# Two attention layers and two feed-forward layers in one kernel: a fourth buffer for transposed contexts, another order of the first loads, and a shorter chain of work before the last layer

## The chip, the cores and the metric

The kernel runs on one core of one Trainium2 chip. The metric is device time in microseconds (us) for one execution; lower is better. The core has TensorE (matmuls, PE in the profile, with its weight loads as PEld), VectorE (DVE), ScalarE (ACT), GpSimd (POOL) and SyncE (SP), which only issues transfers. Each engine works off its own instructions in the order in which the program gives them, and waits on semaphores for what others produce. Transfers are issued by SP, ScalarE and GpSimd, and 16 DMA engines carry them out.

## What is computed

There are 16 batches, each of 112 query rows and 375 context rows of 256 numbers, all in 32-bit floats. Four layers follow one another, each as `x = x + layer(layernorm(x))`:

```python
def _L0_xattn_ref(patch_embed, pixel_embed, Wq, Wk, Wv, Wo, bo):   # 16 heads of 64
    q = patch_embed @ Wq
    k = pixel_embed @ Wk
    v = pixel_embed @ Wv
    ...
    attn = jax.nn.softmax(sim, axis=-1)
    ...
    return out @ Wo + bo
def _L0_ffn_ref(...):                                  # 2 experts, one per row, and a shared one
    top1 = jnp.argmax(gate_probs, axis=-1)
    ...
    h = jax.nn.relu(jnp.einsum('end,edh->enh', masked, w1) + b1[:, None, :])
    expert_out = jnp.einsum('enh,ehd->end', h, w2) + b2[:, None, :]
    ...
    shared = jax.nn.relu(xf @ sw1 + sb1) @ sw2 + sb2
    return (routing_output + shared).reshape(B, S, D)
def _L1_xattn_ref(query, key, value, mask):            # one head of 256, key = value = context
    e = jnp.einsum('bid,bjd->bij', query, key) * scale
    ...
    a = jax.nn.softmax(e, axis=-1)
    return jnp.einsum('bij,bjd->bid', a, value)
def _L1_ffn_ref(x, weight_int8, weight_scale, bias):   # one scale for all of x
    x_scale = jnp.maximum(jnp.abs(x2).max() / 127.0, EPS)
    x_int8 = jnp.clip(jnp.round(x2 / x_scale), -128, 127).astype(jnp.int8)
    ...
    out = acc_i32.astype(jnp.float32) * x_scale * weight_scale.T
```

The last layer needs the largest absolute value over all 16 batches before it can quantize anything.

## The kernel before

The order of all work is written out by hand: a list of units, and for each unit calls that are put in its middle (`mid`) or at its end (`at`). What is issued first on an engine or a queue runs first there.

*The opening* (L137 to L187, L1169 to L1174). SP and ScalarE issue the first loads: x of the first two batches (`load_xb`, 224 KB) and the transposed context of batch 0 (`ctxT`, 375 KB), then the weights wk, wq and wv in quarters of 256 KB (`first_w`). While these come in, TensorE runs `WARM` products of zeros (L182). Then follow the first keys (`make_kT`, L338, L347), the turn of x (`q_turn`, L327, L330), and the first queries (`make_q`, L395).

*The first attention* (units 0 to 63, `unit`). A unit is four heads of one batch. Unit u computes the scores of u (L426), their largest values on VectorE (L434), exponentials on ScalarE (L443), the division on GpSimd (L455), and the keys of unit u + 1. The values of unit u - 2 (`make_v`, L359) are made in unit u, and unit u - 3 gets its weighted sum (L514). So the values of unit 0 are made in unit 2.

*Shared and routed feed-forward.* The shared expert runs in seven chunks of 256 rows (`Rows.run`, L760 for the first layer, L772 on ScalarE and L770 on VectorE for the relu `hT`, L747 for the second layer). For the two experts the rows are sorted into slots of 128 rows, in two halves of the batches. A slot's result is stored in HBM (`slot_store`, L823, tensor y_s) by SP. Rows are gathered back by GpSimd (`sort_get`, L829, tile got) when all slots of the half are stored, and are added to x (L843).

*The last eight batches* (TAIL = 8, batches 8 to 15) go through the second attention after the first has ended. The driver is `stages(k)`. Step k runs the scores of batch 8 + k (`second_2`, L857, tile pe), with the softmax (L862, L871, L872 and L878), the turn of the probabilities (`second_3`, L460), and the weighted sum of the batch two steps behind (`second_4`, L888). The layer norm before it is L271 and L272 on VectorE, L275, L276 and L286 on GpSimd and L300 on ScalarE; the norm after it is followed by a turn (`third_turn`, L327, L330) and the batch's largest value (`third_max`, L925). In the units before step 0, the last chunk of the shared expert, number 6, runs in four parts on TensorE, between the norms of batches 8 and 9. Its result is stored to x2_d by SP (L804), and from there x of batches 13 to 15 is loaded (L809).

Each batch needs two forms of its context: `ctxT2` (L130, transposed, 128 partitions) for the scores and `ctx_nat` (L121, 125 partitions of three rows) for the weighted sum. In this stage `ctxT2` has three buffers and `ctx_nat` five. Pairs 8, 9 and 10 are issued on SP's queue one per unit, each after the store of a slot; the later ones at the end of steps 0 to 4. `x3T` (L1244, 896 KB) brings back what batches 0 to 7 have ready for the last layer, on the same queue.

*The end* (L1328 to L1399). The largest value of batch 15 comes straight from its statistics (`farthest`). It is turned on TensorE (pm), reduced on VectorE (top), spread over all partitions by a product (pb), with two small products between them that keep TensorE going (`keep_warm`). From it come xscale and rscale. Then pairs of batches are scaled (`scaled`, L1355 on ScalarE or L1357 on VectorE), made whole numbers (`products`, L1362), multiplied (L1366), scaled back (L1377), added to x (L1385, on VectorE or GpSimd) and stored by SP (L1386). The tile y has four buffers.

Of the kernel before, what the change touches and what calls it, by code (L numbers as in the profile page):

```python
# [9 lines left out]
F32 = mybir.dt.float32  # L10
# [9 lines left out]
P = 128  # L20
B, S, D = 16, 112, 256
SK = 375
# [4 lines left out]
DC = D // P  # L27
MC = INNER // P
FC = HID // P
GB = 2  # L30
# [11 lines left out]
QB = S // 4  # L42
KB = (SK + 31) // 32
KP = (P, P, SK - 2 * P)
WARM = 4
POOL_PLACES = 7
CROW_PLACES = 4
NT = B * S // P
# [6 lines left out]
TAIL = 8  # L55
# [3 lines left out]
def tile_kernel(  # L59
# [26 lines left out]
    nc = tc.nc  # L86
# [4 lines left out]
    ctxp = ctx.enter_context(tc.tile_pool(name="ctx", bufs=2))  # L91
# [19 lines left out]
    xb = {}  # L111

    def load_xb(g):
        xb[g] = tmp.tile([S, GB, D], F32, tag="xb", name=f"xb_{g}", bufs=1)
        (nc.gpsimd if g else nc.sync).dma_start(out=xb[g], in_=x[:, g * GB : (g + 1) * GB, :])

    ctx_nat, ctxT, ctxT2 = {}, {}, {}

# [5 lines left out]
    def load_ctxT(b, dma=nc.sync):  # L124
        ctxT[b] = ctxp.tile([P, DC, SK], F32, tag="ctxT", name=f"ctxT{b}")
        dma.dma_start(out=ctxT[b], in_=ctx_t[b])

    def load_ctxT2(b):
        ctxT2[b] = late(ctxp, 2, 3, [P, DC, SK], "ctxT_2", f"ctxT2_{b}")
        nc.sync.dma_start(out=ctxT2[b], in_=ctx_t[b])  # L130

    def weight(src, name, dma, pool=wpool):
        t = pool.tile(list(src.shape), F32, tag=name, name=name)
        dma.dma_start(out=t, in_=src)
        return t

    load_xb(0)  # L137
    load_ctxT(0, nc.scalar)
    first_w = {
        n: awpool.tile([P, DC, INNER], F32, tag=n, name=n) for n in ("wk", "wq", "wv")  # L140
    }
    for k in range(UN):
        sl = slice(k * UD, (k + 1) * UD)
        for n, src, dma in (("wk", wk, nc.sync), ("wq", wq, nc.scalar), ("wv", wv, nc.sync)):
            dma.dma_start(out=first_w[n][:, :, sl], in_=src[k])
        if k == 0:

            ones = const.tile([P, P], F32, tag="ones", name="ones")
            nc.vector.memset(ones, 1.0)
            nc.scalar.activation(ones[0:1, 0:1], ones[0:1, 1:2], AF.Identity)  # L150
# [94 lines left out]
    def late(pool, bufs, more, shape, tag, name):  # L245

        pool, bufs = (fin[0], more) if fin else (pool, bufs)
        return pool.tile(shape, F32, tag=tag, name=name, bufs=bufs)
# [86 lines left out]
    def make_kT(b, m, on_act):  # L335
        pk = gen(f"pk_{b}_{m}")
        for dc in range(DC):
            nc.tensor.matmul(  # L338
                pk[:, :SK],
                wk_sb[:, dc, m * P : (m + 1) * P],  # L340
                ctxT[b][:, dc, :],
                start=(dc == 0),
                stop=(dc == DC - 1),
            )
        t = act.tile([P, SK], F32, tag="kT", name=f"kT_{b}_{m}", bufs=2)
        if on_act:
            nc.scalar.copy(t, pk[:, :SK])  # L347
        else:
            nc.vector.tensor_copy(t, pk[:, :SK])
        kT[b, m] = t  # L350
# [562 lines left out]
    def third_turn(bs):  # L913
        for b in bs:
            if b < TAIL:
                t = tmp.tile([P, DC, S], F32, tag="x3s", name=f"x3s_{b}", bufs=1)
                transposed(t, normed["l3", b], f"x3_{b}")
                nc.scalar.dma_start(out=x3T_d[b], in_=t)
            else:
                transposed(x3T[0][:, b, :, :], normed["l3", b], f"x3_{b}")  # L920
# [90 lines left out]
    NU = B * UN  # L1011
# [6 lines left out]
    def at(u, f, *a):  # L1018
        extra[u].append((f, a))
# [142 lines left out]
    for b in range(TAIL, B):  # L1162

        at(FIRST_RUN + 3 if b < 13 else STEP_0 + b - 13, load_xs, b)
    for i in range(3):
        at(STEP_0 - 7 + i, load_ctxT2, TAIL + i)
        at(STEP_0 - 7 + i, load_ctx, TAIL + i)

    make_kT(0, 0, True)  # L1169
    for i in range(GB):  # L1170
        q_turn(0, i)
    make_kT(0, 1, True)
    for m in range(2):
        make_q(0, m)  # L1174

    def unit(u, work=None):
        nb, nk = divmod(u + 1, UN)
        vb, vk = divmod(u - 2, UN)
        has_s = u < NU
        has_k = u + 1 < NU  # L1180
        has_t = 0 <= u - 1 < NU
        has_v = 0 <= u - 2 < NU
        has_w = 0 <= u - 3 < NU
        after_block = u - 1 in blocks
        if has_w and after_block:
            weighted(u - 3)
        if has_t:
            unit_T(u - 1, 0)
            unit_T(u - 1, 1)
        if has_s:  # L1190
            scores(u)
            exps(u, 0)
            exps(u, 1)
        if has_w and not after_block:
            weighted(u - 3)
        if has_t:
            unit_T(u - 1, 2)
            unit_T(u - 1, 3)
            stay = unit_move(u - 1)
        pump(3)  # L1200
        if has_k:
            make_kT(nb, 2 * nk, True)
        if has_s:
            divide(u, 0)
        pump(3)
        if has_v:
            make_v(vb, vk, (0, 1))
        pump(4)
        for f, a in middle[u]:
            f(*a)  # L1210
        if has_s:
            divide(u, 1)
        if work:
            work()
        pump(4)
        if has_k:
            make_kT(nb, 2 * nk + 1, True)
        if has_v:
            make_v(vb, vk, (2,))
        if has_t:  # L1220
            unit_stay(*stay)
        pump(4)
        for f, a in extra[u]:
            f(*a)
            pump(2)

    def keep_warm(count):

        pi = gen("warm")
        for _ in range(count):  # L1230
            nc.tensor.matmul(pi[:, :P], ident, ident, start=True, stop=True)
# [22 lines left out]
    def stages(k):  # L1254
        def b_of(back):
            b = TAIL + k - back
            return b if TAIL <= b < B else None

        def do(back, f):
            b = b_of(back)  # L1260
            if b is not None:
                f(b)

        def norm_steps(name, b):
            nb_on = nc.gpsimd if name == "l2" or b == B - 1 else nc.vector
            steps[name, b] = norm([b], name, True, nb_on)
            for f in steps[name, b][:3]:
                f()

        def now(f, at_k):  # L1270

            for b, own in zip(range(TAIL, B), at_k):
                if own == k:
                    f(b)

        def rows(name):
            return lambda b: steps[name, b][3]()

        no = None
        stats = lambda b: norm_steps("l2", b)  # L1280
        now(sort_get, (-4, -4, -3, -3))
        now(sort_add, (-3, -3, no, no, 1, 2, 3, 4))
        now(stats, (-2,))
        now(rows("l2"), (-1,))
        yield
        now(sort_add, (no, no, -2, -1))
        now(stats, (no, -2))
        if k == -1:
            now(rows("l2"), (no, -1))
            do(-1, second_1)  # L1290
        do(0, lambda b: second_2(b, lambda: do(-1, second_1)))
        do(4, lambda b: third_turn([b]))
        do(1, second_3)
        do(3, rows("l3"))
        now(rows("l2"), (no, no, 0, 1, 2, 3, 4, 5))
        do(2, second_4)
        if k == B - TAIL + 1:

            amax1.append(const.tile([S, 1], F32, tag="amax1", name="amax1"))
            do(3, lambda b: third_max([b]))  # L1300
            nc.vector.tensor_reduce(amax1[0], amax[:, : B - 1], AX.X, ALU.max)
        do(2, lambda b: norm_steps("l3", b))
        now(sort_get, (no, no, no, no, -1, 0, 1, 2))
        now(stats, (no, no, -1, 0, 1, 2, 3, 4))
        if k >= 0:
            do(-3, load_ctxT2)
            do(-3, load_ctx)
        if k != B - TAIL + 1:
            do(3, lambda b: third_max([b]))
        yield  # L1310
# [22 lines left out]
    nc.tensor.transpose(pm[:1, :S], amax1, ident[:S, :S])  # L1333
    top = const.tile([1, 1], F32, tag="top", name="top")
    nc.vector.tensor_reduce(top, pm[:1, :S], AX.X, ALU.max)
    keep_warm(2)
    pb = gen("pb")
    nc.tensor.matmul(pb[:, :1], ones[0:1, :], top, start=True, stop=True)
    xscale = const.tile([P, 1], F32, tag="xscale", name="xscale")
# [11 lines left out]
    def scaled(pair):  # L1351
        t = x3T[0][:, 2 * pair : 2 * pair + 2, :, :]

        if pair % 2 or pair == 6:
            nc.scalar.activation(t, t, AF.Identity, bias=rounding, scale=rscale)  # L1355
        else:
            nc.vector.tensor_scalar(t, t, rscale, ROUND, ALU.mult, ALU.add)  # L1357
# [17 lines left out]
    def stored(pair):  # L1375
        y = fin[0].tile([S, 2, D], F32, tag="y", name=f"y_{pair}", bufs=4)
        nc.vector.tensor_tensor(  # L1377
            y,
            pfs[pair][:S, : 2 * D].rearrange("p (j d) -> p j d", j=2),
            wsx.unsqueeze(1).to_broadcast([S, 2, D]),  # L1380
            ALU.mult,
        )
        first = xs_place[2 * pair]
        add = nc.vector if pair in (2, 5, 7) else nc.gpsimd
        add.tensor_tensor(y, y, xall[:S, first : first + 2, :], ALU.add)  # L1385
        nc.sync.dma_start(  # L1386
            out=out[2 * pair : 2 * pair + 2].rearrange("b s d -> s b d"), in_=y
        )
# [70 lines left out]
```

## Time and profile before

| What | us |
|---|---|
| median of 3 runs (lowest, highest) | 969.3 (968.51, 970.0) |
| the profiled execution, whole time | 970.18 |
| its span, first to last instruction | 968.4 |
| TensorE busy in the span | 925.2 |
| VectorE, ScalarE, GpSimd busy | 494.3, 465.9, 463.8 |
| mean granted TensorE clock | 0.986 |

The page gives each engine's busy time over the whole span, and cuts the span into 40 slices of 24.2 us. The timelines quoted further down have one row for each instruction, or for several merged ones (x4): start in us from the span's start, length in us, engine, line, what it writes and reads, and in brackets how long the engine stood idle before it and what ended that. Rows of SPq are transfers that SP issues; their length is that of the issue, not of the transfer. Rows of stretches give for each engine its busy time in us and, in brackets, its instructions, then the clock granted to TensorE, the share of the 16 DMA engines that was busy, and the GB/s that they moved.

### The profile page before, as it was taken

To read this page: it belongs to the slowest core of one execution; us is meant where nothing else is said; L and a number is where in the kernel's file an instruction comes from. 1 tells how busy PE (TensorE), PEld (TensorE's weight loads), DVE (VectorE), ACT (ScalarE), POOL (GpSimd) and SP (SyncE) were. 2 spreads that over 40 slices of the span, in tenths; PEclk is the share of its full clock that TensorE was granted. 3 is DMA by queue.
4 is the path that set the end of the run, shared out by engine and by line. 5 is a ranking of instruction groups with operands and counts; after the bars stand their busy time and mean duration, and the time that the engine had idled before them with its cause. 6 is when DMAs were issued, how large, how long until landed. Compare 5 with 4: busy or idle time off the path is not lost. (4 is left out here: it accounts for less than half of the span.)

```text
span 968.4 us, 16839 instructions
## 1 busy us (share of the span) xinstructions
PE 925.2 (96%) x5567; PEld 706.4 (73%) x5567; DVE 494.3 (51%) x1276; ACT 465.9 (48%) x1241; POOL 463.8 (48%) x504
## 2 busy tenths in 40 slices
PE   8999999999999999999999999899999999999683
PEld 5677677777777777778778787667767678899462
DVE  5655855464545444653444434577576442322464
ACT  4766565366535554564353442554545641221453
POOL 4766664366536544553242334666555622201743
PEclk9999999999999999999999999999999999999996
DMA  5654543243326422332645522645335720586522
GB/s 185 161 164 95 136 129 74 71 101 92 74 74 197 121 70 52 77 83 59 217 159 179 205 50 70 161 127 139 95 77 133 201 59 30 201 325 220 151 96 76
DMA packets 119911, 120.69 MB, mean 125 GB/s; under 512 B 15807, under 2 KB 107153, under 8 KB 115089
## 3 DMA queue, kind: packets, MB, share of 16 engines
q1 hardware_dynamic: 107664, 97.52, 35.8%
q10 hardware_dynamic: 8144, 11.20, 4.0%
q0 software_dynamic: 4016, 10.90, 3.7%
q8 instruction: 45, 0.74, 0.3%
q14 instruction: 42, 0.34, 0.1%
HBM read 71.19 MB, written 10.62 MB: 84 GB/s over the span
## 5 line engine op out<-in xcount | busy, mean ns | idle before, releaser
L455 POOL TENSOR_SCALAR p<-p,rden 128x375 f32<-128x375 f32 x256 | 315.1, 1244 | 258.4 <-DVE rden L452 251.3
L443 ACT ACTIVATE p<-sc,nmax 128x375 f32<-128x375 f32 x256 | 143.4, 571 | 174.9 <-DVE nmax L434 169.6
L338 PE MATMUL pk<-ctxT,wk 128*128 128x375 f32 x512 | 192.1, 497 | 4.3 <-ACT kT L347 2.3
L359 PE MATMUL pv<-wv,ctxT 128*128 128x256 f32 (+1 forms) x768 | 187.0, 380 | 0.4 <-ACT kT L347 0.4
L359 PEld LDWEIGHTS pv<-wv,ctxT 128*128 128x128 f32 (+1 forms) x768 | 143.3, 187 | 47.9 <-ACT kT L347 1.6
L504 ACT COPY pT<-blk 32x384 f32<-32x384 f32 x256 | 130.0, 508 | 29.2 <-DMA pT<-blk 26.9
L476 DVE STREAM_TRANSPOSE blk<-p 128x384 f32<-128x384 f32 x256 | 132.2, 552 | 7.4 <-POOL p L455 4.5
L338 PEld LDWEIGHTS pk<-ctxT,wk 128*128 128x128 f32 x512 | 90.3, 191 | 55.7 <-issue 9.9
L434 DVE TENSOR_REDUCE nmax<-sc 128x2 f32<-128x750 f32 x128 | 111.8, 911 | 0.6 <-PE sc L426 0.5
L514 PEld LDWEIGHTS pa<-pT,v 128*64 128x64 f32 (+1 forms) x1536 | 74.4, 136 | 33.3 <-issue 15.8
L426 PE MATMUL sc<-kT,qT 64*128 64x375 f32 x512 | 98.1, 501 | 0.0
L514 PE MATMUL pa<-pT,v 128*64 128x112 f32 (+1 forms) x1536 | 88.3, 263 | 2.2 <-DMA pT<-blk 1.4
L372 DVE COPY v<-pv 119x256 f32<-119x256 f32 x64 | 27.0, 423 | 122.5 <-PE pv L359 101.3
L347 ACT COPY kT<-pk 128x375 f32<-128x375 f32 x128 | 61.3, 479 | 47.0 <-PE pk L338 47.0
L426 PEld LDWEIGHTS sc<-kT,qT 64*128 64x128 f32 x512 | 43.9, 186 | 34.1 <-issue 13.5
L770 DVE TENSOR_SCALAR hT_sl<-ph_sl,slot_b 128x128 f32<-128x128 f32 x64 | 22.3, 349 | 69.3 <-PE ph_sl L760 69.3
L760 PE MATMUL ph_sh<-ffn_x,sw 128*128 128x256 f32 x224 | 56.0, 381 | 0.0
L747 PE MATMUL acc_sh<-sw,hT_sh 128*128 128x256 f32 x224 | 55.5, 379 | 0.3 <-ACT hT_sh L772 0.3
L395 PE MATMUL pq<-xT,wq 128*128 128x224 f32 x256 | 54.2, 354 | 0.0
L772 ACT ACTIVATE hT_sl<-ph_sl,slot_b 128x128 f32<-128x128 f32 x64 | 23.2, 367 | 60.6 <-PE ph_sl L760 49.2
L443 ACT ACTIVATION_READ_ACCUMULATOR p<-sc,nmax 128x1 f32 x256 | 51.8, 202 | 0.0
L542 PE MATMUL po<-wo,oT 128*128 128x256 f32 x224 | 50.8, 380 | 0.1
(221 smaller groups left out, 1148.1 us busy)
## 6 DMA issues: line engine op xcount, KB each, us to landing
pT<-blk SPq DMA_DIRECT2D x732, 48.0 KB
ctxT<-in_ctx_t SPq DMA_DIRECT2D x31, 375.0 KB
ctx<-in_ctx SPq DMA_DIRECT2D x16, 375.0 KB
ew<-in_w ACTq DMA_DIRECT2D x2, 1024.0 KB
x_s<-idle POOLq DMA_DIRECT2D x2, 1024.0 KB, 5.8
sw<-in_sw ACTq DMA_DIRECT2D x2, 1024.0 KB
row<-x_s SPq DMA_DIRECT2D x16, 128.0 KB
y_s<-yrow SPq DMA_DIRECT2D x16, 128.0 KB
```

What stands on the lines that cost most here:

```text
L338: nc.tensor.matmul(pk[:, :SK], wk_sb[:, dc, m * P : (m + 1) * P], ctxT[b][:, dc, :], start=(dc == 0), stop=(dc == DC - 1),)
L347: nc.scalar.copy(t, pk[:, :SK])
L359: nc.tensor.matmul(pv[: KP[c], n * UD : (n + 1) * UD], ctxT[b][:, dc, c * P : c * P + KP[c]], wv_sb[:, dc, k * UD : (k + 1) * UD], start=( ...
L426: nc.tensor.matmul(sc[:, j, :SK], qT[g, m][r, i * P : (i + 1) * P], kT[b, m][r, :], start=True, stop=True,)
L434: nc.vector.tensor_reduce(nmax, sc[:, :, :SK], AX.X, ALU.max, negate=True)
L443: nc.scalar.activation(p[:, :SK], sc[:, j, :SK], AF.Exp, bias=nmax[:, j : j + 1], accum_out=den[:, j : j + 1])
L455: nc.gpsimd.tensor_scalar(p, p, rden[:, j : j + 1], None, ALU.mult)
L476: nc.vector.transpose(blocked[u][:, :, h * 32 : (h + 1) * 32], probs[u][h].rearrange("p (n k) -> p n k", k=32),)
L504: nc.scalar.copy(pT[r, :, i, :], of[r, :, i, :])
L514: nc.tensor.matmul(pa[j * DH : (j + 1) * DH, j2 * S : (j2 + 1) * S].rearrange("p (i q) -> p i q", q=QB), vv[b, k][: KP[c], c, h * DH : (h ...
L747: nc.tensor.matmul(self.acc[:n, i, :D], hT[:, i * n : (i + 1) * n], self.wb[:, f, :], start=(f == 0), stop=(f == FC - 1),)
L760: nc.tensor.matmul(ph[:, : self.n], self.wa[:, dc, f * P : (f + 1) * P], self.src[:, dc, :], start=(dc == 0), stop=(dc == DC - 1),)
```

## The change

- The first loads: batch 0's transposed context is loaded in two halves, one by SP and one by ScalarE. Then SP loads the first quarter of wk in two halves; x goes to ScalarE's queue, behind its half of the context. The number of warm-up products (`WARM`) goes from 4 to 3.
- The first unit: both keys come first, then the values of unit 0 (`make_v`), around the turns of x. Unit 2 makes no values any more.
- The contexts of the second attention: `ctxT2` gets four buffers in place of three. Pairs 8 and 9 are issued together, and 10 and 11 one unit later. Step k then loads batch 8 + k + 4 in place of 8 + k + 3. On SP's queue pairs 10 and 11 thereby stand ahead of the store of the last slot, and pair 12 stands where 11 stood.
- The end: batch 14's turn goes from the last step, behind pb, to the step before, ahead of pm. The two `keep_warm` products between top and pb are dropped. ScalarE scales pairs 2 to 7 (before 1, 3, 5, 6 and 7) and VectorE pairs 0 and 1. VectorE adds pairs 4 and 7 (before 2, 5 and 7), and GpSimd the others.

```diff
-WARM = 4
+WARM = 3
...
-        (nc.gpsimd if g else nc.sync).dma_start(out=xb[g], in_=x[:, g * GB : (g + 1) * GB, :])
+        (nc.gpsimd if g else nc.scalar).dma_start(out=xb[g], in_=x[:, g * GB : (g + 1) * GB, :])
...
-        ctxT2[b] = late(ctxp, 2, 3, [P, DC, SK], "ctxT_2", f"ctxT2_{b}")
+        ctxT2[b] = late(ctxp, 2, 4, [P, DC, SK], "ctxT_2", f"ctxT2_{b}")
...
-    load_xb(0)
-    load_ctxT(0, nc.scalar)
+    ctxT[0] = ctxp.tile([P, DC, SK], F32, tag="ctxT", name="ctxT0")
+    for c, dma in enumerate((nc.sync, nc.scalar)):
+        dma.dma_start(out=ctxT[0][:, c, :], in_=ctx_t[0][:, c, :])
     first_w = {
         n: awpool.tile([P, DC, INNER], F32, tag=n, name=n) for n in ("wk", "wq", "wv")
     }
+    for m in range(2):
+        sl = slice(m * P, (m + 1) * P)
+        nc.sync.dma_start(out=first_w["wk"][:, :, sl], in_=wk[0][:, :, sl])
+    load_xb(0)
     for k in range(UN):
         sl = slice(k * UD, (k + 1) * UD)
         for n, src, dma in (("wk", wk, nc.sync), ("wq", wq, nc.scalar), ("wv", wv, nc.sync)):
-            dma.dma_start(out=first_w[n][:, :, sl], in_=src[k])
+            if k or n != "wk":
+                dma.dma_start(out=first_w[n][:, :, sl], in_=src[k])
...
-    for i in range(3):
-        at(STEP_0 - 7 + i, load_ctxT2, TAIL + i)
-        at(STEP_0 - 7 + i, load_ctx, TAIL + i)
+    for i in range(4):
+        at(STEP_0 - 7 + i // 2, load_ctxT2, TAIL + i)
+        at(STEP_0 - 7 + i // 2, load_ctx, TAIL + i)
 
     make_kT(0, 0, True)
+    make_kT(0, 1, True)
+    make_v(0, 0, (0, 1))
     for i in range(GB):
         q_turn(0, i)
-    make_kT(0, 1, True)
+    make_v(0, 0, (2,))
     for m in range(2):
         make_q(0, m)
...
-        has_v = 0 <= u - 2 < NU
+        has_v = 0 < u - 2 < NU
...
-        do(4, lambda b: third_turn([b]))
+        if k < B - TAIL + 2:
+            do(4, lambda b: third_turn([b]))
...
             do(3, lambda b: third_max([b]))
             nc.vector.tensor_reduce(amax1[0], amax[:, : B - 1], AX.X, ALU.max)
+            do(3, lambda b: third_turn([b]))
...
         if k >= 0:
-            do(-3, load_ctxT2)
-            do(-3, load_ctx)
+            do(-4, load_ctxT2)
+            do(-4, load_ctx)
...
-    keep_warm(2)
...
-        if pair % 2 or pair == 6:
+        if pair > 1:
...
-        add = nc.vector if pair in (2, 5, 7) else nc.gpsimd
+        add = nc.vector if pair in (4, 7) else nc.gpsimd
```

## The prediction

> **What bounds the kernel now.** I read the page first: TensorE is busy for 96% of a span of 968.4 us, so time is lost only where TensorE stands or runs at a lower clock. The slices show this in the first, in the last three, and nowhere else.
>
> ```profile
> PE 925.2 (96%) x5567; PEld 706.4 (73%) x5567; DVE 494.3 (51%) x1276; ACT 465.9 (48%) x1241; POOL 463.8 (48%) x504
> PE   8999999999999999999999999899999999999683
> PEclk9999999999999999999999999999999999999996
> ```
>
> Then TensorE's timeline at both ends (start, length, in brackets the idle time and what ended it).
>
> ```profile
> 7.72 1.50 PE L338 MATMUL pk<-ctxT,wk 128*128 128x375 f32 x4 [1.17 <-DMA wk<-in_wk]
> ...
> 919.94 2.81 PE L857 MATMUL pe<-ctxT,xT 128*112 128x375 f32 x4 [5.67 <-DMA ctxT<-in_ctx_t]
> ...
> 925.39 1.43 PE L857 MATMUL pe<-ctxT,xT 128*112 128x375 f32 x4
> ...
> 929.22 1.49 PE L857 MATMUL pe<-ctxT,xT 128*112 128x375 f32 x4
> ...
> 933.18 1.49 PE L857 MATMUL pe<-ctxT,xT 128*112 128x375 f32 x4
> ...
> 945.85 1.09 PE L1231 MATMUL warm<-ident 128*128 128x128 f32 x4
> 946.87 0.58 PE L1338 MATMUL pb<-top,ones 1*128 1x1 f32 x2
> ```
>
> The wait of 5.67 us is batch 12's transposed context. The four pe rows are batches 12 to 15, some 4 us apart at the end. What feeds them is SP's queue:
>
> ```profile
> 880.47 0.35 SPq L823 DMA_DIRECT2D y_s<-yrow  x1
> 880.85 0.43 SPq L130 DMA_DIRECT2D ctxT<-in_ctx_t  x1
> 881.64 0.28 SPq L121 DMA_DIRECT2D ctx<-in_ctx  x1
> 887.49 0.33 SPq L823 DMA_DIRECT2D y_s<-yrow  x1
> ...
> 906.58 0.43 SPq L1244 DMA_DIRECT2D x3T<-x3T_d  x1
> 907.11 3.87 SPq L130 DMA_DIRECT2D ctxT<-in_ctx_t  x1
> ...
> 911.48 4.31 SPq L809 DMA_DIRECT2D x<-x_d  x1
> ```
>
> The last y_s (887.49) is the last expert slot's result, and all gathers (got, L829) wait for it. The last views are GpSimd's and VectorE's timeline, and the stretch 884 to 888 us (busy time of each engine, clock, DMA share, GB/s), in which hardly anything but a context (ctx, L121) moves.
>
> ```profile
> 890.75 0.99 POOL L829 DMA_INDIRECT got<-y_s,batch_place  x1 [56.28 <-issue]
> ...
> 923.70 0.73 POOL L843 TENSOR_TENSOR x<-x,got 112x256 f32<-112x256 f32 x1 [4.20 <-DMA x<-x_d]
> ```
> ```profile
> 896.26 0.43 DVE L271 BATCH_NORM_STATS2 bn_l<-x 112x6 f32<-112x256 f32 x1 [4.48 <-POOL x L843]
> 896.72 0.18 DVE L272 BATCH_NORM_AGGREGATE mv_l<-bn_l 112x2 f32<-112x6 f32 x1
> 896.82 0.45 DVE L770 TENSOR_SCALAR hT_sh<-ph_sh,sb 128x256 f32<-128x256 f32 x1
> ```
> ```profile
> 884.00:888.00 4.00, 4.00 (x24) 3.64 (x23) 1.11 (x3) 0.46 (x2) 0.00 (x0) 1.00 0.34 119
> ```
>
> A context, 375 KB (384,000 bytes) in 125 rows, thus moves at 119 GB/s on 0.34 of 16 engines, about five, and takes 3.2 us. A transposed context of the same size is spread over all 16; a sixteenth of it, 24,000 bytes, at one busy engine's 119 / 5 = 23.8 GB/s takes 1.0 us. So a pair ctxT, ctx costs those five engines 4.2 us, which is the spacing of the last pe rows (3.83 and 3.96 us): the tail of the batch stage is fed at that pace.
>
> The Trainium skill, "DMA: Bandwidth & Descriptors", section "Why a DMA increments its semaphore by 16 and not by 1", says that a transfer takes the largest number of engines up to 16 that divides its slowest dimension, 5 for 125 rows; the share of 0.34 agrees. Its section "Queues, rings and completion order" adds that each engine works a queue's descriptors off in order, so that a short store behind long ones waits for the slowest of its engines. That speaks against this change: by the rule my sum would end at +2.6 us, and if a store passed what stands before it, at -7.0.
>
> **The change, part by part.**
>
> *Contexts, fourth buffer.* Pairs 8 and 9 are now issued together after the store of slot 6 (873.2), pairs 10 and 11 after that of slot 7 (880.47), ahead of the last store. Before, the five engines were busy to about 888 with pair 9 (share 0.34 up to there), and the store of 887.49 found them free: GpSimd was released some 2.4 us later (a first piece of the gather at 889.87). Now pairs 10 and 11 stand before it: 2 x 4.2 = 8.4 us, less the few tenths by which the store came before the engines were free; I take 8.2. A store waiting in this queue isn't shown before. The bounds: 0, if the store passed the contexts, and 8.4, both pairs in full. The nearest row is x of 911.48, 112 KB on the same queue behind a context and 896 KB: GpSimd waited for it until 923.70, 12.2 us from issue. So the upper end.
>
> What that delays: gathers, then x, then bn of batch 8 on VectorE at 896.26. Behind it in VectorE's order stands hT_sh (L770, 896.82), which TensorE's second layer of the shared chunk needs; on ScalarE the next hT_sh stands behind xn in the same way. TensorE has 0.29 us of idle time there (before 899.32), so nothing covers it: the delay goes through, with a stand of about 7.4 us (898.2 to 905.6). After its 5.67 us stand before, TensorE ran at half clock to about 924.2, 4.2 us after its restart. Twelve second-layer matmuls, 2.85 us (1.03 + 1.99 less overlap), would then run at half clock; part of this hides in waiting for hT_sh: 1.4 us. Bounds: 0 (clock back at once) and 2.85. The store of x2_d (902.07), and with it every load behind it, moves by 8.2 + 1.4 = 9.6 us.
>
> What it gains: after x2_d one pair less stands in the queue, since batch 11's pair is in already. Batch 12's context gets the place of batch 11's, and batch 15's that of 14's: pe of batch 15 can run one step earlier, 933.18 - 929.22 = 4.0 us. Not the whole 5.67 plus slow clock: x3T and batch 15's x stay in the same places, and x at 923.70 - after it add, bn, root, xn, turn, some 4 us - would allow pe at about 928, just under the 929.2 that the context allows. Bounds of the gain: 0 and 7.0 (5.67 and half of the 2.81 us slow pe). I take 4.0. Stage: +8.2 + 1.4 - 4.0 = +5.6.
>
> *First loads.* Before, the first product waited for ctxT, x, wk and wq quarters, 375 + 224 + 256 + 256 KB, since two queues share the engines: 1.14 MB. Now: ctxT's halves on both queues, half of wk's quarter (128 KB), and x beside it (224 KB), with some of wq (I put 150 KB): 0.90 MB. The difference, 0.24 MB at 304 GB/s (5 to 6 us), is 0.8 us. The pieces of wk are half as long in a row, and SP has one issue more (0.7 us, while earlier bytes still move): 0.7 us gained. Bounds: 0, and 1.17, the wait in the row. One warm-up product less (5.03 us / 4 = 1.26) costs TensorE nothing, since it waits then; but these ran at 0.63 us each and pk at 0.375, so the clock rose between them, and if it rises later now, products of some 3.4 us run at half speed. Bounds 0 and 1.7 lost; I take 0.2, nearer to the row in which it was up at 7.72. Part: -0.5. x comes later behind ctxT (bn before at 4.71, now about 6), and its chain of 3.1 us to xn ends near 9.5, covered by pk and pv, which run to about 11; without that cover it would cost what it is late.
>
> The Trainium skill, "TensorE: Matmul & The Clock Gate", section "Part 1: The HAM clock gate", wants a busy window of some 3.4 us, free-running, before full clock. Three warm-up products last 3.8 us here, and the rule would make the opening about 1.7 us dearer where the window is missed.
>
> *First unit's values* (L359, 1.89 + 1.02 us) move from unit 2 to the opening, where TensorE had no hole between 7.72 and 12.3 either: 0. Bounds: -0.5 and +0.5 (L347's kT waits of unit 2, about 0.5 each). Their copies on ScalarE (0.61) and VectorE (0.42) move with them, beside TensorE's products.
>
> *End.* Without the warm-up between pm and pb, pb starts behind top (946.35) instead of at 946.87: 0.45 us. Batch 14's turn (pt_x 947.38, x3T 948.05) goes ahead of pm, into TensorE's idle 3.26 us; so ScalarE's xn of batch 15 no longer waits for it (948.29, now 945.7, when nb is there), and xi of pair 0, at 950.52, runs at about 947.95, after VectorE's two scalings. I replayed the last pairs with their row times (xi 0.47, ScalarE scaling 0.65, y 0.69, adds 1.28 on GpSimd and 1.1 to 1.3 on VectorE, y's buffers free 2.33 us after the store): VectorE's last add ends at 960.0 instead of 962.5. ScalarE takes one scaling more (5 to 6) and GpSimd one add more (5 to 6), inside that replay. So -2.5; bounds -0.45 (only the pb step) and -3.2.
>
> **Sum:** +5.6 - 0.5 - 0 - 2.5 = +2.6 us on the profiled execution (970.18 with 1.8 us around its span; that run lies 0.9 above the median). On the median of 969.3 that is 971.9.
>
> **Rivals.**
> *The store isn't held* (faster). If it passes the contexts, or the gathers have slack, the sum is -4.0 - 0.5 - 2.5 = -7.0: 962.3. For it: eleven engines are idle then. Against: x's 12.2 us. The change wins from a delay under 5.6 us (with the clock's 1.4).
> *Only one pair is ahead of the store*, because SP itself is held (it stood 3.87 and 4.31 us at such issues): 4.2 + 1.0 for the clock - 7.0 = -1.8: 967.5.
> *The stage gives nothing back* (slower yet): VectorE's bn of batch 15, waiting for x, blocks the softmax behind it, so the gain of 4.0 is lost: +6.6, 975.9. For it: the 4.20 us wait at 923.70. Against: 1.2 us of slack reckoned above.
> *It doesn't do what it says*: the wait on a context merely passes to batch 13, behind x3T. This is in my sum; alone, without the held store, it is rival one.
>
> **How the numbers follow.** Forecast 0.62, own range 969.6 to 974.0 (clock, opening and end at their bounds in part); store not held 0.14; one pair 0.13; nothing given back 0.11. What can be told from no change is 0.2%, 1.9 us: 967.4 to 971.2. Faster: 0.14 and a third of 0.13, 0.18. Same: the rest of 0.13 and a quarter of the forecast, 0.24. Slower: 0.58. The range 966.5 to 975.0 leaves out the first rival and a part of the last.
>
> **What would show it.** Right: the first got some 8 us after the last y_s is issued, not 3; TensorE idle for 7 us before acc_sh of the shared chunk, half clock after; no wait on ctxT at batch 12, one at 13; the first pk at about 7.0; VectorE's last add some 2.5 us nearer to pe of batch 15. Wrong: got following the store as before, a cold opening, or the batch stage not fed at 4.2 us a pair.

## The result, and the profile after

| | us |
|---|---|
| median after (4 runs: 976.21, 977.16, 979.78, 984.05) | 978.47 |
| median before, same chip | 968.9 |
| ratio, with its 95% interval | 1.0113 [1.0078, 1.0149] |
| profiled execution after, and its span | 977.16, 975.4 |

The change makes the kernel 1.1% slower, 9.6 us by the medians. The forecast had the side right and the time 6.6 us too low; 978.5 lies above its range. The two profiled executions differ by 7.0 us only: that of before is a slow one for its kernel, that of after the second fastest of four.

The page of after: TensorE's clock now has a slice at 8, the third from the end, where the slice of before had 9.

```profile
PE 927.5 (95%) x5561; PEld 705.3 (72%) x5561; DVE 493.5 (51%) x1274; ACT 467.0 (48%) x1242; POOL 463.5 (48%) x505
...
PEclk9999999999999999999999999999999999999896
```

TensorE's timeline after, the rows that answer to those of before (lines have moved by 7 or 8):

```profile
6.56 2.76 PE L345 MATMUL pk<-ctxT,wk 128*128 128x375 f32 x8 [0.92 <-DMA wk<-in_wk]
...
35.46 1.61 PE L521 MATMUL pa<-pT,v 128*64 128x112 f32 x24 [2.39 <-DMA pT<-blk]
...
909.53 5.03 PE L754 MATMUL acc_sh<-sw,hT_sh 128*128 128x256 f32 x12 [7.54 <-DVE hT_sh L777]
915.19 1.52 PE L864 MATMUL pe<-ctxT,xT 128*112 128x375 f32 x4 [0.43 <-ACT xT L337]
...
937.96 1.52 PE L864 MATMUL pe<-ctxT,xT 128*112 128x375 f32 x4 [1.97 <-DVE nmax L878]
...
942.79 1.43 PE L864 MATMUL pe<-ctxT,xT 128*112 128x375 f32 x4
...
956.04 0.58 PE L1348 MATMUL pb<-top,ones 1*128 1x1 f32 x2 [0.35 <-DVE top L1346]
```

The first keys start 1.16 us earlier (7.72 before), of which a part is chance: see the section on the prediction. The wait of 2.39 us for transposed probabilities at 35 us is new. So is the stand of 7.54 us ahead of the shared expert's second layer (0.29 before), after which twelve products take 5.03 us: half clock. The wait of 5.67 us for batch 12's context is gone; batch 15's scores (942.79) come 9.61 us later than before (933.18).

SP's queue after, and the gather that follows:

```profile
884.29 1.74 SPq L830 DMA_DIRECT2D y_s<-yrow  x1
...
886.93 4.18 SPq L130 DMA_DIRECT2D ctxT<-in_ctx_t  x1
...
891.60 3.51 SPq L830 DMA_DIRECT2D y_s<-yrow  x1
```
```profile
902.97 0.99 POOL L836 DMA_INDIRECT got<-y_s,batch_place  x1 [64.85 <-DMA y_s<-yrow]
```

The last slot's store is issued at 891.60 behind pairs 10 and 11, and even its issue takes 3.51 us (0.33 before). The gather starts 11.4 us after the issue began; before it was 3.3 us (887.49 to 890.75). The chain of waits names the same transfer and, 33 us on, a second one of the same kind, x of batch 15 behind batch 13's context:

```profile
891.60 10.40 DMA y_s<-yrow
...
924.80 10.81 DMA x<-x_d
```

### The profile page after: what moved, and what is told of

Same layout as the page of the kernel before. It is cut to its first block, busy times and chain, and to the rows that moved or that the text cites. A ratio compares the mean times of both kernels' runs of the same rounds, so it can differ in the third digit from the quotient of the medians.

```text
span 975.4 us, 16831 instructions
## 1 busy us (share of the span) xinstructions
PE 927.5 (95%) x5561; PEld 705.3 (72%) x5561; DVE 493.5 (51%) x1274; ACT 467.0 (48%) x1242; POOL 463.5 (48%) x505
## 5 line engine op out<-in xcount | busy, mean ns | idle before, releaser
L483 DVE STREAM_TRANSPOSE blk<-p 128x384 f32<-128x384 f32 x256 | 132.1, 551 | 11.2 <-DMA pT<-blk 5.7
L345 PEld LDWEIGHTS pk<-ctxT,wk 128*128 128x128 f32 x512 | 90.5, 191 | 55.3 <-issue 10.3
L754 PE MATMUL acc_sh<-sw,hT_sh 128*128 128x256 f32 x224 | 57.5, 390 | 7.5 <-DVE hT_sh L777 7.5
L754 PEld LDWEIGHTS acc_sh<-sw,hT_sh 128*128 128x128 f32 x224 | 43.7, 196 | 14.7 <-DVE hT_sh L777 7.9
```

The source lines that it names most:

```text
L345: nc.tensor.matmul(pk[:, :SK], wk_sb[:, dc, m * P : (m + 1) * P], ctxT[b][:, dc, :], start=(dc == 0), stop=(dc == DC - 1),)
L483: nc.vector.transpose(blocked[u][:, :, h * 32 : (h + 1) * 32], probs[u][h].rearrange("p (n k) -> p n k", k=32),)
L754: nc.tensor.matmul(self.acc[:n, i, :D], hT[:, i * n : (i + 1) * n], self.wb[:, f, :], start=(f == 0), stop=(f == FC - 1),)
```

## The experiments

Sixteen kernels ran, each timed beside the kernel before on the same chip. The last column is the difference of the medians in us.

| label | what it is | ratio to before | us |
|---|---|---|---|
| e1 | change, values of unit 0 back in unit 2 | 1.0101 [1.0061, 1.0141] | +9.7 |
| e2 | change, pairs 10 and 11 behind the last store | 1.0041 [1.0019, 1.0064] | +4.6 |
| e3 | e1 and e2 together | 1.0011 [0.9993, 1.0029] | +2.2 |
| e4 | change, late contexts cut by rows | 1.0000 [0.9981, 1.0018] | +0.1 |
| e5 | change, four idle products | 1.0136 [1.0113, 1.0160] | +12.2 |
| e6 | e1 with four idle products | 1.0089 [1.0070, 1.0107] | +8.9 |
| e7 | e6 with the cut contexts | 0.9995 [0.9984, 1.0006] | -1.1 |
| e8 | e7 with pairs 10 and 11 behind the store | 0.9952 [0.9940, 0.9964] | -5.4 |
| e9 | e8 with the early values | 0.9984 [0.9966, 1.0002] | -2.5 |
| e10 | before with cut contexts alone | 0.9967 [0.9948, 0.9986] | -3.1 |
| e11 | before with the end's edits alone | 0.9980 [0.9967, 0.9993] | -2.0 |
| e12 | e8 with three idle products | 0.9957 [0.9943, 0.9971] | -3.7 |
| e13 | before with the context edits alone | 1.0115 [1.0089, 1.0141] | +10.3 |
| e14 | before with first loads and warm-up alone | 1.0003 [0.9988, 1.0018] | -0.6 |
| e15 | before with the early values alone | 1.0029 [1.0016, 1.0042] | +2.7 |
| e16 | e8 with three context buffers, old schedule of pairs | 0.9953 [0.9935, 0.9971] | -3.8 |

### Opening or context stage?

The first four were built on the changed kernel. Their edits:

```diff
# e1
-    make_v(0, 0, (0, 1))
...
-    make_v(0, 0, (2,))
...
-        has_v = 0 < u - 2 < NU
+        has_v = 0 <= u - 2 < NU
# e2 (e3 is both)
-        at(STEP_0 - 7 + i // 2, load_ctxT2, TAIL + i)
-        at(STEP_0 - 7 + i // 2, load_ctx, TAIL + i)
+        at(STEP_0 - 7 + min(i, 2), load_ctxT2, TAIL + i)
+        at(STEP_0 - 7 + min(i, 2), load_ctx, TAIL + i)
# e4
-        nc.sync.dma_start(out=t, in_=ctx_in[b].rearrange("(c p) d -> p c d", p=KC))
+        of = ctx_in[b].rearrange("(c p) d -> p c d", p=KC)
+        if b < TAIL:
+            nc.sync.dma_start(out=t, in_=of)
+        else:
+            for r in (slice(0, S), slice(S, KC)):
+                nc.sync.dma_start(out=t[r], in_=of[r])
```

> The changed kernel with one part undone: the values of unit 0 are made in unit 2 again, as before the change. Main theory: the early values push the first probabilities' transposes back by 1.6 us and leave unit 2 without work that hides the wait for them, which lets the TensorE clock fall at 36 to 40 us; with the part undone unit 0's scores start near 11.2 us (13.93 in the changed kernel), the wait on the transposed probabilities in unit 2 is at most 0.5 us, the scores of units 5 to 39 start about 4 us earlier than in the changed kernel (1.2 us earlier than in the kernel before), and the time is about 4 us under the changed kernel's, near 973 to 974. Rival, that the new order of the first loads or the shorter warm-up is at fault: the scores of units 5 to 39 still start 2 us or more later than in the kernel before, and the time stays within 1.5 us of the changed kernel's.

> The changed kernel with the four context buffers kept, but the loads of pairs 10 and 11 issued behind the last slot's store instead of ahead of it. Main theory: the store of the last slot's outputs leaves the queue before those pairs, the first gather lands within 3 us of it, the stand of 7.5 us at the shared weights' products goes down to under 1 us, and no context is late for batches 9 to 15; the time is 6 to 9 us under the changed kernel's, near 969 to 971. Rival, that the stand comes from the gathers or the x loads in the other queues: the stand keeps 4 us or more and the time falls by under 3 us. Second rival, that the wait passes on to the contexts: TensorE waits for a context in batches 9 to 13 for 4 us or more, and the time falls by under 5 us.

> The changed kernel with both parts undone: the values of unit 0 in unit 2, and pairs 10 and 11 behind the last slot's store. If the two losses stand in different stages and don't touch each other, their gains add up: 10 to 13 us under the changed kernel, 963 to 967 us, which is below the kernel before. Rival, that one gain swallows the other or that the rest of the change costs time as well: 968 us or more.

> The changed kernel with the ten late context loads cut in two by rows, 0 to 111 and 112 to 124, in the same queue and the same order. Main theory: a load of 125 rows lands on five DMA engines alone, which makes a pair take 4.2 us; the part of 112 rows spreads over more engines, a pair takes 2 to 2.5 us, the last slot's store lands 3 to 4 us sooner, and the time is 3 to 4 us under the changed kernel's. Rival, that the queue is bound by its issues: two more issues of about 0.6 us each stand ahead of the store, and the time is the same or 1 to 2 us above.

*e1*: the wait for transposed probabilities went and the unit that followed ran at full clock, but the time stayed, and unit 0's scores started at 14.15 us instead of near 11.2. The view of the tile pk (instructions, shortest, median and longest in ns, first and last start) shows why, for the change, then for e2:

```profile
L345 PE MATMUL pk<-ctxT,wk x8: 476/478/553, 6.6 to 8.8; 128*128 128x375 f32 x8
```
```profile
L345 PE MATMUL pk<-ctxT,wk x8: 480/832/966, 6.2 to 10.5; 128*128 128x375 f32 x8
```

In e1, e2 and e3 most of the first eight products (five in e1, six in e2 and e3) take 830 ns or more instead of 478: half clock, which cost 1.7 us in e1 (4.41 us for the eight, 2.76 in the change) and 2.1 in e2 (4.85).

*e2* took 5.0 us off the change, *e3* 7.4 (by the last column against +9.6). The stand at acc_sh fell to 1.1 and 1.2 us, but 1 us or more of the gain expected was missing in e2, some 3 in e3, so that all three expectations were missed. In the profile of e2 a part is the half clock of the opening (unit 63's scores start 1.5 us later than in the change). The rest is here (TensorE, then GpSimd):

```profile
933.15 2.84 PE L864 MATMUL pe<-ctxT,xT 128*112 128x375 f32 x4 [2.79 <-DVE nmax L878]
```
```profile
930.93 0.72 POOL L850 TENSOR_TENSOR x<-x,got 112x256 f32<-112x256 f32 x1 [4.11 <-DMA x<-x_d]
```

Batch 14's scores wait, because VectorE's norm of batch 15 waits for x, and batch 13's maxima (nmax), for which the row says these scores wait, stand behind it. That x (batch 15's, not 14's as an expectation below has it) stands on SP's queue behind x3T and pairs 12 and 13, as it does in the change. The second rival was right that a wait would be left, but it is one for x and not for a context, and it was there before: 1.97 us in the change.

*e4* changes neither the order nor the buffers, and took 9.4 us off, more than twice what was expected: the stand fell from 7.5 to 1.5 us, and the wait at batch 14's scores from 1.97 us to 0.63. Rival "bound by its issues" is out. The issues tell it too: with one issue more in each pair, SP's longest between the stores takes 1.06 us in e4, against 4.18 in the change.

### Once more the opening, and the contexts on top

```diff
# e5: on the change; e6: on e1; e7: e6 with e4's edit; e8: e7 with e2's edit
-WARM = 3
+WARM = 4
```

> The changed kernel with the warm-up back at four idle matmuls (eight records instead of six). Theory W, that the shorter warm-up leaves the clock on the edge so that in some executions the first products run at half clock (480 ns each in the changed kernel's profile, about 830 ns in the profiles of the two runs with the values or the stores moved): the eight first products take under 3.2 us, the scores of unit 0 start between 13.6 and 14.3 us, and the median is 0.5 to 2.5 us under the changed kernel's. The wait of TensorE for the transposed probabilities of unit 0, 1.8 to 2.4 us near 35 us, stays, because the early values stay. Rival, that the half clock comes from the idle time ahead of the first products and not from the warm-up's length: products above 700 ns show here too. Rival, no effect: the median within 0.5 us of the changed kernel's.

> The changed kernel with two parts undone: the values of unit 0 made in unit 2 again, and four idle matmuls in the warm-up. Theory W plus early values: the first products take under 3.2 us, the scores of unit 0 start at 11.6 to 12.5 us (14.15 with the values alone moved back), no wait of 1 us or more for transposed probabilities between 30 and 40 us, and the scores of units 5 to 39 start 0.8 us earlier to 0.2 us later than in the kernel before (2.75 later in the changed kernel). The stand at the shared weights' products stays at 7 to 8 us; the time is 2 to 4 us under the changed kernel's. Rival, that the new order of the loads itself costs 1.5 us or more: the scores of units 5 to 39 start 1.5 us or more later than in the kernel before.

> As the run before (values in unit 2, four idle matmuls), and the late context loads cut in two by rows as in the run that fell by 9 us. If the two gains are apart: units 5 to 39 start no later than in the kernel before, the stand at the shared weights' products is 1 to 2 us, and the time is 1 to 3 us under that run, 965.5 to 967.5. Rival, that the stand grows again as the stages before it become earlier, because it hangs on the landing of the loads and not on the engines: the time stays at 968 or above.

> As the run before, with pairs 10 and 11 issued behind the last slot's store as well. If a stand is left that the two pairs ahead of the store make, it goes: 0 to 2 us under the run before, 964 to 967. Rival, that the wait passes on to the x rows of batch 14, which are issued behind those pairs in the same queue (TensorE waited 2.2 to 2.8 us for their maxima in the two runs with the store ahead): a wait of 1.5 us or more there, and the time the same as the run before or above it.

*e5* and *e6* put the opening right: first products at 478 and 480 ns, unit 0's scores at 14.35 and 12.67 us, and in e6 units 5 to 39 only 0.34 us later than before (2.75 in the change). Yet e5 is slower than the change, if anything, and e6 can't be told from it. Both missed. Against each other they price the early values: e6 is 3.3 us faster than e5, and their intervals are apart. In e6's profile the last scores of the first attention start 4.4 us earlier than in the change, and batch 15's 1.0 us later. In this execution, what the opening gained is lost in the context stage:

```profile
906.68 5.69 PE L754 MATMUL acc_sh<-sw,hT_sh 128*128 128x256 f32 x12 [8.88 <-DVE hT_sh L777]
...
932.86 2.81 PE L864 MATMUL pe<-ctxT,xT 128*112 128x375 f32 x4 [2.81 <-DMA ctxT<-in_ctx_t]
```

*e7* and *e8* take that stage's brake away. e8's queue at the same place as the change's above, then the stretch 888 to 892 us of the change, then of e8 (clock, DMA share, GB/s at the end):

```profile
887.02 0.34 SPq L835 DMA_DIRECT2D y_s<-yrow  x1
...
888.87 0.35 SPq L135 DMA_DIRECT2D ctxT<-in_ctx_t  x1
889.26 0.92 SPq L126 DMA_DIRECT2D ctx<-in_ctx  x2
```
```profile
888.00:892.00 4.00, 4.00 (x24) 3.64 (x23) 0.93 (x3) 0.64 (x2) 0.00 (x0) 1.00 0.51 167
```
```profile
888.00:892.00 4.00, 4.00 (x20) 3.51 (x20) 0.97 (x2) 0.47 (x1) 1.94 (x2) 1.00 0.93 262
```

With whole contexts half of the 16 engines work while the store waits; cut, nearly all do. The 0.51 is a mixture of contexts and transposed contexts; a context nearly alone had 0.34 (884 to 888 us in the kernel before), about five engines. The Trainium skill, "DMA: Bandwidth & Descriptors", section "Why a DMA increments its semaphore by 16 and not by 1", gives the number of engines as the largest up to 16 that divides the rows: 5 for 125, 16 for 112, 13 for 13. The shares of 0.34 for a whole context and 0.93 after the cut agree with it.

e8 is the fastest of all kernels here: 963.53 us, 0.48% [0.36, 0.60] under the kernel before. In e7, where pairs 10 and 11 still stand ahead of the store, TensorE stands 2.65 us at acc_sh, in e8 0.69, and no scores wait for x in either. So e7 stayed above what was expected (967.81 us; a stand of 1 to 2), and e8 went beyond it, 4.3 us under e7.

### One part alone

```diff
# e9: e8 with the change's make_v and has_v; e12: e8 with WARM = 3; e10: before with e4's edit
# e11: before with the diff's part from third_turn to the end
# e16: e8 with before's ctxT_2 buffers and schedule of pairs
# e13: before, and
+        ctxT2[b] = late(ctxp, 2, 4, [P, DC, SK], "ctxT_2", f"ctxT2_{b}")
...
+    for i in range(4):
+        at(STEP_0 - 7 + i // 2, load_ctxT2, TAIL + i)
+        at(STEP_0 - 7 + i // 2, load_ctx, TAIL + i)
...
+            do(-4, load_ctxT2)
+            do(-4, load_ctx)
# e14: before with the diff's first loads and WARM = 3; e15: before with the diff's make_kT, make_v and has_v
```

> The fastest run so far (late context loads cut by rows, pairs 10 and 11 behind the last slot's store, values of unit 0 in unit 2, four idle matmuls) with the early values of the change put back alone. Theory: with the context queue no longer setting the end, the opening counts in full: the early values delay unit 0's scores by about 2 us, save 3.3 us in unit 2 and lose 2 to 4 us to the wait for the transposed probabilities in unit 3, so the scores of units 5 to 39 start 0.7 to 2.2 us later than in that run, and the time is 0.7 to 2.5 us above it: 964 to 966. Rival, that what the opening loses is swallowed later, as it was in the runs whose context loads were whole: within 0.6 us of that run.

> The fastest run so far with three idle matmuls instead of four, as in the change. Theory W, the clock on the edge: where the first eight products run at half clock, unit 0's scores start at about 14.1 us and units 5 to 39 start about 2 us later than in that run; where they don't, at 11.5 to 12.0 us; the median is 0.3 to 2 us above that run. Rival, that the shorter warm-up is free or a gain: the median is the same or up to 0.5 us below, and the first products take under 3 us.

> The kernel before with nothing changed but the late context loads cut in two by rows. If a context of 125 rows is slow because it lands on few DMA engines, TensorE's wait of 5.67 us for the context of batch 12 goes down to 2 to 4 us, and the time is 2 to 4 us under the kernel before's: 965 to 967. Rival, that this wait hangs on the third buffer coming free: the wait stays above 5 us and the time is within 0.7 us of the kernel before's.

> The kernel before with the change's edits of the end alone (order of the last turn, the two idle matmuls taken out, the scaling and the last additions given to other engines). As predicted: the stretch from batch 15's first products to the end is 2.0 to 3.0 us shorter (35.25 us in the kernel before) and the time is 2 to 3 us under the kernel before's: 966 to 967. Rival, that the gain needs the fourth buffer: under 1 us.

> The kernel before with the change's context edits alone: fourth buffer, two pairs in each of the two steps ahead of the last slot's store, the later pairs one step earlier. Theory, that the stage was under-sized in the prediction because hardly anything is given back behind the stand when the stage is reached on time: 9 to 13 us above the kernel before, 977.5 to 982; batch 15's first products 8 us or more later than in the kernel before. The prediction's own term: 5.6 us above, 973 to 975.5, with 3.5 to 4 us of the stand given back between batch 8's and batch 15's first products.

> The kernel before with the new order of the first loads and the warm-up of three idle matmuls alone. The prediction's term: 0.5 us under the kernel before (0.7 gained, 0.2 for the risk of a half clock), 967.5 to 968.5, first products of the keys from 6.5 us on at 480 ns each. Theory W, the clock on the edge: in executions with products near 830 ns the scores of unit 0 start at 13.5 us or later and the median is 0.5 to 1.5 us above the kernel before.

> The kernel before with the early values of unit 0 alone. The prediction's term: no change (within 0.5 us). Theory, that the values delay the first scores by their own 2.9 us and leave unit 2 without the work that covered the wait for the transposed probabilities: unit 0's scores start at 14.5 to 15.5 us, the transposed probabilities are waited for 1.4 us or more near 35 us, units 5 to 39 start 0.5 to 3 us later than in the kernel before, and the time is 1.5 to 3 us above it.

> The fastest run so far with three context buffers and the kernel before's schedule of the pairs (so: the kernel before with the cut loads, the new order of the first loads and the edits of the end). If the gains of the cut loads (3.1), the end (2.0 to 2.5) and the opening (0.3) add up: 963 to 964, the same as with four buffers, and the fourth buffer is worth nothing. Rival, that the fourth buffer still takes away the wait of 2.2 us for the context of batch 12: 1 to 2.5 us above the fastest run's ratio to the kernel before, 964.5 to 966.

*e9* and *e15* price the early values twice more, in kernels whose context stage is not jammed: 2.5 us by the medians on top of e8 (on two chips; 2.9 by the last column), 2.7 us [1.6, 4.1] on top of the kernel before. e15, opening and units 2 and 3:

```profile
9.05 1.89 PE L359 MATMUL pv<-wv,ctxT 128*128 128x256 f32 x8
...
13.82 1.53 PE L426 MATMUL sc<-kT,qT 64*128 64x375 f32 x8
...
34.08 1.38 PE L514 MATMUL pa<-pT,v 128*64 128x112 f32 x24 [1.47 <-DMA pT<-blk]
```

The kernel before, units 2 and 3:

```profile
26.66 1.89 PE L359 MATMUL pv<-wv,ctxT 128*128 128x256 f32 x8
31.92 1.02 PE L359 MATMUL pv<-wv,ctxT 128*119 128x256 f32 x4
34.33 1.38 PE L514 MATMUL pa<-pT,v 128*64 128x112 f32 x24
```

There the values stand ahead of pa, and pa doesn't wait. e15's first scores start 7.37 us after its first keys product (13.82 - 6.45), against 4.61 in the kernel before (12.33 - 7.72): later by 2.8 us, the length of the values. SP moves the transposed probabilities one by one, and the first of these moves starts 9.40 us after the first scores in both kernels (23.22 in e15, 21.73 before), so the whole chain is later; and with the values gone from unit 2, TensorE reaches pa and waits. The time and the wait came as expected; unit 0's scores (13.82, not 14.5 or later) and units 5 to 39 (0.33 us later, not 0.5) did not, since the first product of this execution starts 1.3 us earlier than in the profile of before. Reckoned from the first product, the loss by unit 5 is some 1 us; where the rest of the 2.7 us falls is open.

*e12*: its profile shows no half clock, and the median lies 1.35 us above e8's, which ran on another chip; the ratios' intervals overlap. Inconclusive as a time. Over all 18 profiles, though, three idle products left the first keys at half clock in 3 of 7, four in none of 11 (two had a single slow product). The Trainium skill, "TensorE: Matmul & The Clock Gate", section "Part 1: The HAM clock gate (the "warmup" mystery)", says that the window is free-running, so that the same kernel can warm up at different points; 3 of 7, in kernels with the same warm-up, agrees.

*e10* met its expectation: batch 12's wait 2.19 us instead of 5.67, 3.1 us gained. The last rows of pe in e10 (batches 13 to 15):

```profile
921.03 1.43 PE L862 MATMUL pe<-ctxT,xT 128*112 128x375 f32 x4
...
924.75 1.43 PE L862 MATMUL pe<-ctxT,xT 128*112 128x375 f32 x4
...
928.57 1.43 PE L862 MATMUL pe<-ctxT,xT 128*112 128x375 f32 x4
```

*e11* met its expectation too: batch 15's scores to the end takes 32.79 us (35.25 before), 2.0 us gained.

*e13* is the term of the prediction's sum that weighed most, alone: 10.3 us by the medians, where 5.6 were predicted. Its profiled execution was the fastest of five (976.23) and ends only 6.1 us later than the profile of before, with batch 15's scores 6.2 us later (8 or more were expected) and the stand predicted:

```profile
906.93 4.54 PE L747 MATMUL acc_sh<-sw,hT_sh 128*128 128x256 f32 x12 [8.24 <-DVE hT_sh L770]
```

The four other executions took 1.2 to 6.5 us longer than this one, and no profile of this kernel shows where.

*e14* is the kernel before within its interval. *e16* has the ratio of e8 (by the medians, on two chips, e8 gains 1.6 us more): with short loads the fourth buffer is worth nothing that can be told from the spread.

## Why the prediction was wrong

Four profiles have the context stage of before (before, e11, e14, e15), five that of the change (the change, e1, e5, e6, e13). Their means, in us:

| stretch | before | change | difference | predicted |
|---|---|---|---|---|
| unit 63's scores to the first got | 116.3 | 125.4 | +9.1 | +8.2 |
| first got to batch 8's scores | 11.2 | 12.6 | +1.4 | +1.4 |
| batch 8's to batch 15's scores | 30.7 | 28.7 | -2.0 | -4.0 |
| all three | 158.2 | 166.7 | +8.5 | +5.6 |

*Held store: right,* at 9.1 us where 8.2 were taken. The store waits behind two pairs at five engines' pace, SP's issue and all, and got, hT_sh, the half clock and x2_d follow as the prediction traced them. The first got, 11.4 us behind the issue, fits its sum (3.3 + 8.2), not its sign of "some 8 us". The rivals "store isn't held" (962.3) and "only one pair is ahead" (967.5) fall with the 7.5 us stand.

*Given back 4.0: the step that failed in this stage.* Against the mean of 30.7 the five give back 3.1 (the change), 3.0 (e1), 0.4 (e5), 0 (e6) and 3.5 (e13), 2.0 in the mean. (A part of the gap is the profile of before, which had caught a long wait for batch 12: 5.67 us, against 4.17, 3.88 and 4.00 in e11, e14 and e15.) Two readings behind the 4.0 don't hold. The first is that the last scores are fed at the contexts' pace of 4.2 us a pair. In e10, with cut contexts and no wait for one behind batch 12, they are still 3.72 and 3.82 us apart, so their spacing isn't that pace. The second is the way from batch 15's x to its scores, "some 4 us". In the change it takes 7.05 us from the add of x (935.74) to the scores (942.79); in e1, e6 and e13 7.0, in e5 8.6. GpSimd, then VectorE:

```profile
935.74 0.72 POOL L850 TENSOR_TENSOR x<-x,got 112x256 f32<-112x256 f32 x1 [3.05 <-DMA x<-x_d]
```
```profile
936.50 0.43 DVE L278 BATCH_NORM_STATS2 bn_l<-x 112x6 f32<-112x256 f32 x1 [3.06 <-POOL x L850]
...
937.36 0.54 DVE L878 TENSOR_REDUCE nmax<-pe 112x1 f32<-112x375 f32 x1
```

Batch 13's maxima stand behind the norm of batch 15 in VectorE's order. With them batch 14's scores are held (937.96), and batch 15's come one step of 4.83 us after those. That uses up the slack of 1.2 us, so x sets the time and not the context, and x comes late: 10.81 us from issue in the change, 20.2 to 20.7 us behind batch 8's scores in the change, e1 and e13, 21.8 and 23.7 in e5 and e6, which give back least. The rival "nothing given back" (975.9) named this mechanism, VectorE's norm of batch 15 waiting for x, and was nearer the truth than the forecast; the whole stage costs 8.5 us, 2.9 more than the sum had: 2.0 here and 0.9 in the hold.

*First unit's values, 0 with bounds of 0.5: wrong,* and the other step that failed: they cost 2.7 us (2.5 and 3.3 in the other two comparisons). The prediction looked for holes in TensorE and found none, so it called the move free. It didn't ask what starts late when the first scores do (SP's moves of transposed probabilities, one chain through the first units), nor what the values covered in unit 2.

*First loads, -0.5:* the first keys did start earlier, at 6.5 us in the mean of the 13 profiles with the new order (6.04 to 6.98) and 7.1 in the five with the old (6.45 to 7.72): 0.6 us, with 0.7 predicted. But the risk of the half clock, priced at 0.2 us, is 3 in 7 times 1.9 us (1.7 and 2.1 in e1 and e2), 0.8. So the term comes to +0.2, and e14's time can't be told from 0.

*End, -2.5: right.* The stretch behind batch 15's scores is 32.3 to 32.9 us in all 13 profiles with these edits and 34.3 to 35.3 in the others, 2.4 us more in the mean; e11's time gives -2.0 [-3.2, -0.7].

Together, with -2.2 for the end: 8.5 + 2.7 + 0.2 - 2.2 = 9.2, against 9.6 measured. Of the 7.0 us between the sum of 2.6 and that, 2.9 are in the context stage, 2.7 in the values, 0.7 in the loads and 0.3 at the end. How near this comes is in part luck: by the times of the parts alone it is 10.3 (e13) + 2.7 (e15) - 0.6 (e14) - 2.0 (e11) = 10.4, and e13's interval alone reaches from 8.6 to 13.7.

Nor do the losses add up in every kernel. Without the early values e6 is 3.3 us faster than e5, yet it can't be told from the change; e1 can't either, where the half clock (1.7 us in its profile) may hide most of the gain. That a stage which is reached earlier loses more is not shown: e13's profile reaches it at 775.2 us and loses least, e6's at 774.2 and loses most. That stage is also where the executions with the change's contexts spread: from unit 63's to batch 15's scores it takes 158.0 to 158.5 us in the four profiles of before's stage, 164.1 to 169.6 in the five of the change's.

One smaller reading of the prediction is incomplete: the slices of before have another 8, the 26th, where "nowhere else" is said. Nothing of the change lies there.

## What to carry to other kernels

A load that lands on few DMA engines sets the pace of its whole queue, of the issuing engine too: cut it into rows that spread (9.4 us on the changed kernel, 3.1 on the kernel before, for six lines) before buying it buffers, whose worth could then not be told from nothing. A piece of work moved into a full stretch of the busiest engine is not free because that engine had no hole: ask what starts later behind it, and which wait it used to cover. When a load comes late, follow what stands behind its first reader in that engine's order: here another batch's work, which made 4 us into 7. And read a term that rests on one wait from more than one execution, if others with the same stage can be had.

## What was not expected of the hardware

- SP's issue of a transfer, mostly 0.3 to 0.5 us in this stage, took 1.7 to 4.6 us behind whole contexts in the change; in e8, with the contexts cut, none up to the pairs behind the last store took over 0.5 us.
- The granted clock in the profile did not show the half clock at the start: in e2 the stretch from 8 to 10 us, below, has 1.00 (third number from the end) while four products fill it. The trace of e2 has no record of the clock before its rise at 10.40 us (10.30 in e1, 10.57 in e3, 4.4 to 7.6 in the others), and the view shows 1.00 where there is none. The length of the products tells the clock there.

```profile
8.00:10.00 2.00, 2.00 (x4) 1.01 (x3) 0.16 (x1) 0.47 (x1) 0.00 (x0) 1.00 1.09 361
```

Open are two small things: from unit 62's scores to unit 63's it takes 12.2 to 13.3 us in the other profiles and 11.93 in that of before, and the step from unit 50 to 51 takes about 19.0 or 17.4 us, in kernels of either kind.
